# One fixed order for VectorE's steps of a slot, and another block for a held product, in a two-layer convolution-attention kernel

## The chip, the cores and the metric

The kernel runs on one core of one Trainium2 chip. The metric is the device time of one execution in microseconds, the median of several runs.

## The reference, cut to what matters

The input is x of 2 x 512 x 32 x 32, in float32. Layer 0 is an attention over 64 sampled positions in each of 8 groups of channels, with a bias from a small network on the distance between the query's place and the sampled place, and then an MLP. Layer 1 is a plain attention over the 1024 places of each image.

```python
# layer 0
q   = gconv1x1(bn(x), qw)
off = tanh(off_pw @ gelu(depthwise 6x6, stride 4, of q)) * 4      # 8 x 8 sampling points
kv  = grid_sample(bn(x), points moved by off);  k, v = gconv1x1(kv, kw), gconv1x1(kv, vw)
pos  = grid_q[:, :, None, :] - grid_kv[:, None, :, :]             # 16 (b, group) x 1024 x 64 x 2
bias = sign(pos) * log1p(abs(pos))
bias = relu(bias @ cpb_w1 + cpb_b1)                               # 2 -> 128
bias = relu(bias @ cpb_w2 + cpb_b2)                               # 128 -> 128
bias = bias @ cpb_w3 + cpb_b3                                     # 128 -> 1
attn = softmax(q k^T / 8 + bias);  x = x + out_w @ (attn v) + out_b
x = x + mlp_w2 @ gelu(mlp_w1 @ bn2(x) + mlp_b1) + mlp_b2          # 512 -> 2048 -> 512
# layer 1
q, k, v = x Wq^T + bq, x Wk^T + bk, x Wv^T + bv
x = x + (softmax(q k^T / sqrt(512)) v) Wp^T + bp
```

The part that takes most of the time is the bias network: 2 x 8 x 1024 x 64 pairs go through its 128 x 128 layer.

## The kernel before, in words

The program is written as one stream of calls. A scheduler of the framework puts them into an order for each engine by its own estimate of what is ready when; `tc.issue_after(i)` adds an edge, so that what is issued inside it stands behind instruction `i`. Each engine then runs its own stream in order.

**The slots.** The bias network is cut into NS = 256 slots, NSL = 16 of them for each of NG = 16 groups (image, chunk of channels, half). A slot is four positions times 1024 queries. Its functions are these:

- `load_tables` (L645) loads a table `fb` of 512 KB for four slots by a DMA on SyncE, and `st_tables` (L656, L664) makes `ta` and `tb` from it on ScalarE: the first layer's two terms.
- `st_layer1(s)` (L676) is the first layer: one custom VectorE instruction adds the terms and clips at zero, and gives `h` of 128 x 4096. There are three buffers of it; slot s issues that of s+2.
- `st_layer2(s)` (L693) is the 128 x 128 layer on TensorE: four tiles, z = 0 to 3, each with 8 matmuls of the program into a PSUM tile from a pool of three. ScalarE evicts them with a relu: z 0 and z 2 to `rx` (L703, three buffers), z 3 to `ub` (L705, three buffers), and z 1 (L705) to a buffer that goes by the slot's place in eight: `u8` (four buffers) for place 0, `u4` (two) for place 4, `uc` (two) for places 2 and 6, `uo` (three) for odd ones. The page calls u8 and u4 both `u`.
- `st_sum(s, 0)` and `st_sum(s, 2)` (L713) are sums on VectorE, `ub = rx * sc + ub`, 128 x 1024 each: of z 0 and 1, and of z 2 and 3. The second also issues on GpSimd's queue an adding DMA of the one into the other (L715).
- Folds, copies and joins (L732 on GpSimd's queue, L739 on SyncE's) bring the sums of two, four and eight slots together, at slots that the table `due` holds.
- `st_layer3` (L823) is the last layer, on TensorE, for all sums of a group into `sim`: for the groups that start at slots 0 to 192 it is issued 27 slots after the group's start, and reads u8 buffers; for those that start at 208 and 224 it is issued 22 slots after, at slots 230 and 246, and reads u8 and u4 buffers; that of 240 follows the loop.
- `softmax_steps` (L836 to L876) are the softmax of a group, in pieces, and `later()` gives the pieces of the chains that prepare the tables of later chunks (`CHAINS`, five of them): one piece in a slot, behind an eviction.

The loop (L886 to L940) issues in each slot, in this order: the second sum of slot s-1, the folds and joins that are due, a table's load, `st_layer1(s + 2)`, `st_layer2(s)`, a table, the first sum of slot s, and then background pieces. No edge orders VectorE's h and sums among themselves.

**The MLP.** After the loop come the output projection (`project`, L1020) and the MLP in eight units, four parts of the hidden width for each of two images. All of its products are made by a scheme of seven products of half size in place of eight. In `layer1` the scheme is used twice: `twice` (matmuls at L160) runs three sets of seven products, one after another, by times: product number q of set g has the time 7g + t, with t from `STEPS`, and calls given as `fills` stand among them by their own times. The seven blocks of `hm` (128 x 2 x 512 each) hold the results: blocks 0 to 3 `c11, c12, c21, c22`, block 4 `r5`, block 5 `r3`; set 0 goes to blocks 0 and 1, set 1 to 2 and 3, set 2 to 4 and 5. The last products are added by `plus` (L137) on VectorE, their copies and scalings are ScalarE's (L166, L170 and their like), and `gelu` (L1092) is ScalarE's. Block 6 is written by the last `spread` of `layer1`, after all sets. One product of the scheme is made plainly, in `second` (time 21), from PSUM into c11. In the first unit (`early`) it is made ahead of all sets, in `first` (time -1), and held in `r3` until `plus(c11, c11, r3)` at time 13.5; the gelu of c11 follows at 19.5. `layer2` (L1073) then multiplies hm by the second weights.

Of the kernel before, what the change touches and what calls it, by code (L numbers as in the profile page):

```python
# [57 lines left out]
def conv_seq_kernel(ctx: ExitStack, tc: tile.TileContext, x, xt, kst, pst, cst, vec, wsm, outw, w1, w2, wl, wlt, brow, out):  # L58
    nc = tc.nc
# [4 lines left out]
    def newest(engine):  # L64
        return next(i for i in reversed(nc.cur_bb.bb.instructions) if i.engine == engine)
# [70 lines left out]
    def plus(out, a, b_, op=ALU.add):  # L136
        nc.vector.tensor_tensor(out, a, b_, op)  # L137
# [69 lines left out]
    with tc.tile_pool(name="lp", bufs=2) as lp:  # L207
# [426 lines left out]

        NS = NG * NSL
        tabs, h1s, sums, sims, added = {}, {}, {}, {}, {}
        evicted, raw = {}, {}


        def load_tables(c):  # L640
            b, k, f = groups[c // 4]
            ci, kk = chain_of[b, k]
            assert ci in state
            fb = lp.tile([P, 2, W, KT], F32, name="fb", bufs=1)
            nc.sync.dma_start(  # L645
                out=fb.rearrange("p a x j -> p (a x j)"),
                in_=fdr[ci][f * len(CHAINS[ci]) + kk, c % 4].rearrange("p j -> (p j)").partition_broadcast(P),
            )
            raw[c] = fb
# [18 lines left out]
        def st_layer1(s):  # L668
            ta, tb = tabs[4 * s // KT]
            j = 4 * s % KT  # L670
            h1 = lp.tile([P, H, 4, W], F32, name="h1", bufs=3)
            a = ta[:, j : j + 4, :].rearrange("p t x -> p (t x)")
            b = tb[:, j // 4].rearrange("p y t -> p (y t)")
            step = H // 2 if s == 0 else H
            for y in range(0, H, step):
                nc.vector._custom_dve(  # L676
                    TENSOR_ADD_SAT,
                    out=h1[:, y : y + step].rearrange("p y t x -> p (y t x)"),
                    in0=a.unsqueeze(1).to_broadcast([P, step, 4 * W]),
                    in1=b[:, 4 * y : 4 * (y + step)].unsqueeze(2).to_broadcast([P, 4 * step, W]),  # L680
                    s0=FMAX, s1=0.0,
                )
            h1s[s] = h1


        def st_layer2(s):
            h1 = h1s.pop(s)
            r = []
            for z in range(4):
                ps = zp.tile([P, 2, 512], F32, name="ps2")  # L690
                for h in range(2):
                    for q in range(4):
                        nc.tensor.matmul(  # L693
                            ps[32 * q : 32 * q + 32, h, :], cw2[:, 32 * z : 32 * z + 32],
                            h1[:, 16 * h : 16 * h + 16, q, :], start=True, stop=True,
                        )
                name, bufs = (
                    ("rx", 3), (("u8", 4), ("uo", 3), ("uc", 2), ("uo", 3), ("u4", 2), ("uo", 3), ("uc", 2), ("uo", 3))[s % 8],
                    ("rx", 3), ("ub", 3),
                )[z]  # L700
                o = lp.tile([P, 2, 512], F32, name=name, bufs=bufs)
                if z % 2 == 0:
                    nc.scalar.activation(o, ps, AF.Relu, bias=sc[:, 4 + z : 5 + z])  # L703
                else:
                    nc.scalar.activation(o, ps, AF.Relu, bias=sc[:, 4 + z : 5 + z], scale=sc[:, z : z + 1])  # L705
                r.append(o)
                if z % 2 == 1:
                    evicted.setdefault(s, []).append(nc.cur_bb.bb.instructions[-1])
            sums[s] = r

        def st_sum(s, z):
            r = [t.rearrange("p h n -> p (h n)") for t in sums[s][z : z + 2]]
            nc.vector.scalar_tensor_tensor(r[1], r[0], sc[:, z : z + 1], r[1], ALU.mult, ALU.add)  # L713
            if z == 2 and s < NS - 1:
                nc.gpsimd.dma_start(out=sums[s][1], in_=sums[s][3], accum_op=ALU.add)  # L715
                added[0] = nc.cur_bb.bb.instructions[-1]
# [167 lines left out]
        st_layer1(0)  # L884
        st_layer1(1)
        for s in range(NS):  # L886
            if s > 0:
                st_sum(s - 1, 2)
            for _, go, a in sorted(due.get(s, ()), key=lambda e: e[0]):
                go(a)  # L890
            if s % 4 == 0 and s // 4 + 1 < 4 * NG:
                load_tables(s // 4 + 1)
            if s + 2 < NS:
                st_layer1(s + 2)
            st_layer2(s)


            if s % 4 == 0 and s // 4 + 1 < 4 * NG:
                with tc.issue_after(evicted[s][0]):
                    st_tables(s // 4 + 1)  # L900
            st_sum(s, 0)

            if bg is not None and (s % 4 or s < 60):
                with tc.issue_after(evicted[s][1]):
                    next(bg, None)
            if bg is not None and state.get(len(CHAINS) - 1, 0) is None:

                bg = None
                php.__exit__(None, None, None)
                opp = tc.tile_pool(name="op", bufs=1, side="right")  # L910
                op = opp.__enter__()
                op0 = op_blocks(
                    0, op.tile([P, 3, 2, 512], F32, name="op0x"), op.tile([P, 3, 2, 256], F32, name="op0w")
                )
                ready = s
            if bg is None and s > ready and (s - ready) % 4 == 0 and (s - ready) // 4 <= 8:
                i = (s - ready) // 4 - 1
                if i < 4:
                    spread(op0[1], (i,))
                else:  # L920
                    fold(nc.vector, op0[0], which=(i - 4,))

            if tails and (s % (2 if s < 60 else 4) or s >= NS - NSL):
                with tc.issue_after(evicted[s][s % 4 == 0]):
                    if next(tails[0], 0) is not None:
                        tails.pop(0)
            for t in (27, 22):
                if s % NSL == t % NSL and s >= t and (s - t < FULL) == (t == 27):
                    st_layer3(s - t)
                    tails.append(softmax_steps((s - t) // NSL))  # L930
# [37 lines left out]
    with ExitStack() as top, tc.tile_pool(name="wp", bufs=1) as wp:  # L968
# [120 lines left out]
        def layer1(p, we, w, xb, xe, hm, others=(), early=False):  # L1089
            def gelu(blk, src, scale=1.0):  # L1090
                for m in range(2):
                    nc.scalar.activation(  # L1092
                        hm[:, blk, m, :], src[:, m, :], AF.Gelu,
                        bias=col("mb1", 4 * p + 2 * (blk // 2) + m), scale=scale,
                    )

            c11, c12, c21, c22, r5, r3 = (hm[:, j] for j in range(6))

            def weights(q, j):
                a = FIRST_W[PARTS[q][0]]  # L1100
                return [inner_w(w, we, a, a - 1)[j]]

            def moving(q, j):
                b_ = FIRST_X[PARTS[q][1]]
                return [inner_x(xb, xe, b_, b_ - 1)[j]]

            def dest(g, m, h):
                return hm[:, 2 * g : 2 * g + 2, m, 256 * h : 256 * h + 256]

            def done(g):  # L1110
                if g == 0:
                    plus(c12, c12, c11)
                elif g == 1:
                    plus(c22, c22, c12)
                    plus(c21, c21, c22)
                    gelu(2, c21, -1.0)
                else:
                    plus(c22, c22, r5)
                    gelu(3, c22, -1.0)
                    plus(c12, c12, r5)  # L1120
                    plus(c12, c12, r3)
                    gelu(1, c12)

            def second():
                ps = mq.tile([P, 2, 512], F32, tag="ps2", name="sw")
                product(w, xb)(ps, 0, 0)
                plus(c11, c11, ps)
                gelu(0, c11)

            def first():  # L1130
                ps = mq.tile([P, 2, 512], F32, tag="ps2", name="sw")
                product(w, xb)(ps, 0, 0)
                nc.scalar.copy(r3, ps)

            plain = ((21, second),)
            if early:
                plain = (-1, first), (13.5, lambda: plus(c11, c11, r3)), (19.5, lambda: gelu(0, c11))
            twice(mq, ((1, 6), (4, 7), (5, 3)), weights, moving, dest, done, (*plain, *others))
            spread([hm[:, j] for j in range(7)])

# [52 lines left out]
        for i, (b, p) in enumerate(units):  # L1193
# [10 lines left out]
            hm = cp.tile([P, 7, 2, 512], F32, tag="big", name="hm")  # L1204
# [387 lines left out]
```

## Time and profile before

| | us |
|---|---|
| median of 3 runs | 2620.16 |
| lowest, highest | 2619.61, 2620.79 |
| the profiled execution, its own time | 2620.51 |
| its span | 2618.7 |
| TensorE's matmuls busy | 2596.1 (99%) |
| VectorE busy | 2310.0 (88%) |
| ScalarE busy | 1746.8 (67%) |
| GpSimd busy | 981.0 (37%) |
| mean granted TensorE clock | 0.999 |

The span is the stretch from the first to the last instruction in the record of the profiled execution; 1.8 us of the execution lie around it. A group of instructions is written as line, engine, operation, out<-in with partitions x elements, count, then busy time in us, mean ns of one, and the idle time of the engine just before them with what ended most of it. A row of the waits says which engine at which line waited for which, the sum in us, how many times, and the longest. A row of the timeline has the start, the duration in us, the engine, the line and the operation, and in brackets the idle time ahead of it and who ended it. One matmul of the program shows as two in the records of the slots. In the trace, slot 228 starts on TensorE at 1683.93 us, slot 232 at 1715.02, slot 246 at 1814.76, and slot 255 at 1882.82.

### The profile page before, as it was taken

To read this page: it belongs to the slowest core of one execution; us is meant where nothing else is said; L and a number is where in the kernel's file an instruction comes from. 1 tells how busy PE (TensorE), PEld (TensorE's weight loads), DVE (VectorE), ACT (ScalarE), POOL (GpSimd) and SP (SyncE) were. 2 spreads that over 40 slices of the span, in tenths; PEclk is the share of its full clock that TensorE was granted. 3 is DMA by queue.
4 is the path that set the end of the run, shared out by engine and by line. 5 is a ranking of instruction groups with operands and counts; after the bars stand their busy time and mean duration, and the time that the engine had idled before them with its cause. 6 is when DMAs were issued, how large, how long until landed. Compare 5 with 4: busy or idle time off the path is not lost.

```text
span 2618.7 us, 48901 instructions
## 1 busy us (share of the span) xinstructions
PE 2596.1 (99%) x19648; PEld 1003.4 (38%) x19648; DVE 2310.0 (88%) x1462; ACT 1746.8 (67%) x2325; POOL 981.0 (37%) x1121
## 2 busy tenths in 40 slices
PE   9999999999999999999999999999999999999999
PEld 3332322233233233323333332332355665646556
DVE  7999999999999999999999999998876587666656
ACT  5887888888887888888887777777733242314041
POOL 1344544444445444444454444333332334200100
PEclk9999999999999999999999999999999999999999
DMA  5888988999899998899898999787787768400202
GB/s 188 173 192 187 212 183 183 195 199 199 190 193 193 187 205 196 179 192 198 187 202 176 201 191 192 164 182 170 150 210 166 153 140 172 94 16 1 73 0 57
DMA packets 177522, 428.27 MB, mean 164 GB/s; under 512 B 29936, under 2 KB 78208, under 8 KB 174608
## 3 DMA queue, kind: packets, MB, share of 16 engines
q0 software_dynamic: 107392, 273.09, 58.2%
q1 hardware_dynamic: 69472, 151.75, 17.5%
q8 instruction: 155, 2.54, 0.4%
q14 instruction: 71, 0.58, 0.1%
q10 hardware_dynamic: 432, 0.31, 0.0%
HBM read 82.16 MB, written 6.55 MB: 34 GB/s over the span
## 4 chain that ended last, share of the span: by engine, by line
PE 67%; DVE 12%; issue 9%; DMA 6%; POOL 4%; ACT 2%; DVEq 0%; SPq 0%; POOLq 0%; ACTq 0%
PE ps L693 39%; PE sw L1073 7%; PE sw L160 7%; PE sw L1242 7%; DVE h L676 4%; DMA u<-uc 3%; DVE ub L713 2%; POOL u L732 2%; PE sw L1020 2%; PE sw L1340 2%; PE psg L595 1%; DVE uo L713 1%; DMA u<-uo 1%; PE sim L823 1%; DMA u<-u 1%
## 5 line engine op out<-in xcount | busy, mean ns | idle before, releaser
L693 PE MATMUL ps<-h,cw 128*32 128x512 f32 x16384 | 1775.4, 593 | 11.1 <-ACT rx L703 7.9
L676 DVE CUSTOM_DVE_ANT_1 h<-ta,tb 128x4096 f32<-128x4096 f32 (+1 forms) x257 | 1130.5, 4400 | 20.6 <-PE ps L693 16.8
L693 PEld LDWEIGHTS ps<-h,cw 128*32 128x32 f32 x16384 | 525.9, 110 | 1229.7 <-issue 1132.2
L703 ACT ACTIVATE rx<-ps,sc 128x1024 f32<-128x1024 f32 x512 | 568.2, 1110 | 158.0 <-PE ps L693 99.1
L732 POOL DMA_DIRECT2D u<-u x397 | 410.0, 1516 | 14.5 <-DMA u<-ub 12.0
L705 ACT ACTIVATE ub<-ps,sc 128x1024 f32<-128x1024 f32 x256 | 308.3, 1204 | 84.1 <-PE ps L693 82.4
L713 DVE SCALAR_TENSOR_TENSOR ub<-rx,sc,ub 128x1024 f32<-128x1024 f32 x256 | 326.7, 1276 | 10.5 <-ACT ub L705 10.5
L715 POOL DMA_DIRECT2D uo<-ub x127 | 112.1, 883 | 586.0 <-DVE ub L713 538.6
L1073 PE MATMUL sw<-hm,w2t 128*128 128x512 f32 x448 | 194.4, 593 | 0.3 <-DVE hm L125 0.2
L705 ACT ACTIVATE uo<-ps,sc 128x1024 f32<-128x1024 f32 x128 | 154.1, 1204 | 42.7 <-PE ps L693 41.3
L713 DVE SCALAR_TENSOR_TENSOR uo<-rx,sc,uo 128x1024 f32<-128x1024 f32 x128 | 163.4, 1277 | 5.0 <-ACT uo L705 5.0
L732 POOL DMA_DIRECT2D u<-uc x126 | 126.9, 1272 | 19.5 <-DMA u<-uc 18.3
L715 POOL DMA_DIRECT2D uc<-ub x64 | 56.3, 879 | 200.6 <-DVE ub L713 159.7
L1073 PEld LDWEIGHTS sw<-hm,w2t 128*128 128x128 f32 x448 | 84.8, 190 | 104.4 <-issue 97.4
L137 DVE TENSOR_TENSOR hm<-hm,sw 128x512 f32<-128x512 f32 x79 | 57.6, 732 | 74.1 <-PE sw L160 51.7
L715 POOL DMA_DIRECT2D u<-ub x64 | 55.1, 860 | 172.0 <-DVE ub L713 168.2
L732 POOL DMA_DIRECT2D uc<-uc x63 | 108.5, 1722 | 2.1 <-DMA uc<-ub 2.1
L732 POOL DMA_DIRECT2D uc<-uo x63 | 103.3, 1639 | 15.3 <-DMA uc<-uo 15.3
L1406 POOL DMA_DIRECT2D xs<-rs x6 | 7.2, 1200 | 258.6 <-DVE rs L137 258.6
L732 POOL DMA_DIRECT2D u<-uo x63 | 87.3, 1386 | 19.4 <-DMA u<-uo 14.8
L705 ACT ACTIVATE uc<-ps,sc 128x1024 f32<-128x1024 f32 x64 | 77.0, 1203 | 24.5 <-PE ps L693 18.0
L656 ACT ACTIVATE ta<-fb,vs 128x512 f32<-128x512 f32 (+1 forms) x65 | 88.7, 1368 | 6.6 <-DMA fb<-fdr 6.6
(295 smaller groups left out, 2622.4 us busy)
## 6 DMA issues: line engine op xcount, KB each, us to landing
uo<-ub POOLq DMA_DIRECT2D x127, 512.0 KB, 5.3
fb<-fdr SPq DMA_DIRECT2D x64, 512.0 KB, 5.8
u<-ub POOLq DMA_DIRECT2D x64, 512.0 KB, 6.5
uc<-ub POOLq DMA_DIRECT2D x64, 512.0 KB, 6.0
u<-u POOLq DMA_DIRECT2D x63, 256.0 KB, 6.9
u<-uo SPq DMA_DIRECT2D x63, 256.0 KB, 5.9
u<-uo POOLq DMA_DIRECT2D x63, 256.0 KB, 7.4
uc<-uc POOLq DMA_DIRECT2D x63, 256.0 KB, 8.2
```

Source lines behind the costliest of these rows:

```text
L137: nc.vector.tensor_tensor(out, a, b_, op)
L160: nc.tensor.matmul(bank[:, e, :], w, x, start=(q in (1, 2, 5) and e == k == 0), stop=True, skip_group_check=True,)
L656: nc.scalar.activation(ta.rearrange("p j x -> p x j")[:, :, j0:j1], fb[:, 0, :, j0:j1], AF.Identity, bias=col("cb1"), scale=col("w1x"),)
L676: nc.vector._custom_dve(TENSOR_ADD_SAT, out=h1[:, y : y + step].rearrange("p y t x -> p (y t x)"), in0=a.unsqueeze(1).to_broadcast([P, ste ...
L693: nc.tensor.matmul(ps[32 * q : 32 * q + 32, h, :], cw2[:, 32 * z : 32 * z + 32], h1[:, 16 * h : 16 * h + 16, q, :], start=True, stop=True,)
L703: nc.scalar.activation(o, ps, AF.Relu, bias=sc[:, 4 + z : 5 + z])
L705: nc.scalar.activation(o, ps, AF.Relu, bias=sc[:, 4 + z : 5 + z], scale=sc[:, z : z + 1])
L713: nc.vector.scalar_tensor_tensor(r[1], r[0], sc[:, z : z + 1], r[1], ALU.mult, ALU.add)
L715: nc.gpsimd.dma_start(out=sums[s][1], in_=sums[s][3], accum_op=ALU.add)
L732: nc.gpsimd.dma_start(out=out, in_=in_, accum_op=ALU.add)
L1073: nc.tensor.matmul(ps[:, m, :], w[:, a, k, m * P : (m + 1) * P], x[:, b_, k, :], start=(k == 0), stop=(k == 1),)
L1242: nc.tensor.matmul(ps[:, m, :], w[:, a, k, c + m * P : c + (m + 1) * P], x[b_][:, k, :], start=(k == 0), stop=(k == nk - 1),)
```

## The change

In the loop, `st_layer1(s + 2)` is issued first and the second sum of slot s-1 after it; the three steps of a slot on VectorE, h of s+2, second sum of s-1, first sum of s, are chained by edges, each behind the newest of them. The edges concern VectorE's order alone. In the first MLP unit the held product goes to block 6 of hm and not to block 5; the plus and the gelu of c11, at times 13.5 and 19.5 before, become one call at time 21.

```diff
@@ the loop over the slots
         for s in range(NS):
+            if s + 2 < NS:
+                with tc.issue_after(summed[-1]) if summed else nullcontext():
+                    st_layer1(s + 2)
+                    summed.append(newest(mybir.EngineType.DVE))
             if s > 0:
-                st_sum(s - 1, 2)
+                with tc.issue_after(summed[-1]):
+                    st_sum(s - 1, 2)
+                    summed.append(newest(mybir.EngineType.DVE))
...
-            if s + 2 < NS:
-                st_layer1(s + 2)
             st_layer2(s)
...
-            st_sum(s, 0)
+            with tc.issue_after(summed[-1]):
+                st_sum(s, 0)
+            summed.append(newest(mybir.EngineType.DVE))
@@ layer1
             def first():
                 ps = mq.tile([P, 2, 512], F32, tag="ps2", name="sw")
                 product(w, xb)(ps, 0, 0)
-                nc.scalar.copy(r3, ps)
-
-            plain = ((21, second),)
-            if early:
-                plain = (-1, first), (13.5, lambda: plus(c11, c11, r3)), (19.5, lambda: gelu(0, c11))
+                nc.scalar.copy(hm[:, 6], ps)
+
+            def merge():
+                plus(c11, c11, hm[:, 6])
+                gelu(0, c11)
+
+            plain = ((-1, first), (21, merge)) if early else ((21, second),)
```

More of the change, by code (lines that the diff above doesn't have):

```diff
@@ L636, in conv_seq_kernel @@
         tabs, h1s, sums, sims, added = {}, {}, {}, {}, {}
-        evicted, raw = {}, {}
+        evicted, raw, summed = {}, {}, []
         def load_tables(c):
```

## The prediction

> **What bounds the kernel now.** I read the engines' busy time first, then the costliest groups, then TensorE's waits.
>
> ```profile
> PE 2596.1 (99%) x19648; PEld 1003.4 (38%) x19648; DVE 2310.0 (88%) x1462; ACT 1746.8 (67%) x2325; POOL 981.0 (37%) x1121
> ...
> L693 PE MATMUL ps<-h,cw 128*32 128x512 f32 x16384 | 1775.4, 593 | 11.1 <-ACT rx L703 7.9
> L676 DVE CUSTOM_DVE_ANT_1 h<-ta,tb 128x4096 f32<-128x4096 f32 (+1 forms) x257 | 1130.5, 4400 | 20.6 <-PE ps L693 16.8
> ...
> L713 DVE SCALAR_TENSOR_TENSOR ub<-rx,sc,ub 128x1024 f32<-128x1024 f32 x256 | 326.7, 1276 | 10.5 <-ACT ub L705 10.5
> ```
>
> TensorE is the bound: 2596.1 of 2618.7 us. A slot's 64 matmuls take 1775.4 / 256 = 6.94 us. VectorE does one h (4.40) and two sums (1.28 each by their rows; 1.20 by start to start, since they overlap by about 0.08) in a slot: 6.75 us, or 97%. So TensorE sets the pace, and VectorE, once late, gains back only some 0.15 us a slot. The waits of TensorE say how little is to be had:
>
> ```profile
> PE ps L693 <- ACT rx L703: 7.9, 14, 1.9
> ...
> PE ps L693 <- DVE h L676: 1.4, 2, 0.7
> PE sw L160 <- ACT hm L166: 1.2, 1, 1.2
> ```
>
> The first two rows are 9.3 us, and TensorE's timeline places 3.5 us of them at two spots: 1713.7 (0.71) and 1808.1 to 1831.0 (0.54, 1.89, 0.70); by the pitch of matmul starts, where 0.425 us is the usual step, these and two smaller gaps are about 1.1 and 3.6, together 4.7 us. The last row is one stall at 1962.4, in the first MLP unit. VectorE's timeline shows the first spot:
>
> ```profile
> 1684.18 4.43 DVE L676 CUSTOM_DVE_ANT_1 h<-ta,tb 128x4096 f32<-128x4096 f32 x1 [0.91 <-PE ps L693]
> 1688.53 1.28 DVE L713 SCALAR_TENSOR_TENSOR ub<-rx,sc,ub 128x1024 f32<-128x1024 f32 x1
> 1691.05 4.43 DVE L676 CUSTOM_DVE_ANT_1 h<-ta,tb 128x4096 f32<-128x4096 f32 x1 [1.25 <-PE ps L693]
> ...
> 1708.74 1.28 DVE L713 SCALAR_TENSOR_TENSOR u<-rx,sc,u 128x1024 f32<-128x1024 f32 x1 [1.14 <-ACT u L705]
> 1710.45 8.76 DVE L676 CUSTOM_DVE_ANT_1 h<-ta,tb 128x4096 f32<-128x4096 f32 x2 [0.43 <-ACT tb L664]
> ```
>
> These are slots 228 to 233. The line at 1708.74 is the sum of z 0 and 1 of slot 228, owed since about 1690, and 1710.45 is h of slots 232 and 233, for which TensorE waits at 1714.3. Why that sum is so late, ScalarE and TensorE tell:
>
> ```profile
> 1707.50 1.21 ACT L705 ACTIVATE u<-ps,sc 128x1024 f32<-128x1024 f32 x1 [0.74 <-PE sim L823]
> ```
>
> The eviction of slot 228's z 1 goes into one of only two u4 buffers, and waits until layer 3 of group 208 (L823, 1705.53 to 1707.45) has read what slot 212 left in it. The same happens at slot 244 (eviction at 1824.76, released by L823 of group 224). These are the only two: earlier groups read only u8 in layer 3.
>
> [...] nothing is put ahead of the sum at 1708.74, and the two h start right after it and the table. [...]
>
> **The change, part by part.** No instruction is added or removed in the loop. The fixed order is h(s+2), sum ub(s-1), sum of z 0,1 of s. I compared the built order of both kernels on each engine. On VectorE they differ at the start, slots 56 to 60, 110 to 115, 143, 164, 227 to 240 and 243 to 255; everywhere else it was this order already.
>
> *Slots 227 to 240.* Before: h230, ub227, h231, ub228, uo229, ub229, uc230, ub230, u4 of 228, h232. After: h230, ub227, **u4 of 228**, h231 and so on. A step that waits for a buffer now stands four sums and one h earlier, and all of VectorE queues behind it. TensorE's and ScalarE's streams move to suit: layer 3 of group 208 starts after slot 229, not 230, split around tile 230.0, and the eviction of u4 stands ahead of rx of 229.2. I walked it with the trace's durations (a tile 1.72 us, 0.25 from a tile's end to its eviction, eviction 1.1 to 1.2, a layer-3 matmul pair of the source 0.21): ub227 ends 1689.8; slot 229 ends on TensorE 1697.7; five layer-3 steps to 1698.75; tile 230.0 waits for the PSUM tile that ub of 229.3 leaves at 1699.15, ends 1700.87; the three u4 steps end 1701.5; eviction 1701.75 to 1702.96; the sum starts at 1703.0. VectorE idles 1689.8 to 1703.0 = 13.2 us. Before, between the same two h it idled 1.25 + 1.29 + 2.44 + 2.15 + 1.14 + 0.43 = 8.7 us. So +4.5 us of VectorE, at 97% load. Of this 0.5 is eaten by the sums that still were owed before: h236 ends at 1737.8 instead of 1734.97 with one more sum owed, about 4.0. TensorE has no slack to swallow it, as slot 232 waited for h already: slot 232 starts at about 1718.6, not 1715.02 (+3.6), slot 234 at 1733.4, not 1729.48 (+3.9).
>
> *Slots 243 to 255.* The same with u4 of 244: idle of VectorE 1811.9 to 1822.4, 10.5 us, against 7.9 before (+2.6). Slot 248 starts 0.7 us later still (+4.7 in all); of that 0.5 comes back, since the stall of 0.53 at 1880.1 is covered. End of loop about **+4.2**. So the 4.7 us of stalls there aren't saved; they become about 8.7. Bounds of the two together: -4.7 (both stalls vanish) to +7.1 (4.5 + 2.6, nothing absorbed).
>
> *Slots 56 to 60.* h runs ahead of ub and uo by one step: a sum comes 4.4 us later, and with it the release of its rx buffer (of three). TensorE loses about **+0.6** (0 to 1.2). *110 to 115:* a stall of about 1.2 is worked out, but the three stalls that follow it in before (0.5, 0.26, 0.4) go in exchange: **0** (0 to +0.6). *Start, 143, 164:* one pair of steps changes places where VectorE was ahead; 0, hidden by h two slots ahead; uncovered, at most one sum, 1.2 us.
>
> *DMAs that move with the sums.* The POOL add of ub into u4 (L715, 0.88 us of issue, 6.5 to land) of 228 and 244 goes ahead of those of uo and uc; one table load on SP changes places with two copies of 256 KB. Their next readers are the copies and joins seven slots (48 us) on, and a table one chunk ahead: 0, hidden. Uncovered: the joins behind land later, one add each, up to 2 x 1.5 us.
>
> *MLP unit 0.* The copy of the first product goes to block 6 instead of block 5, so the copy of the third set (L166, blocks 4 and 5) need not wait for the plus that reads block 5 (1961.48, 1.22 us). The stall of 1.16 us (1.38 by pitch) goes. No plus or gelu is added. But the q7 scaling of set 2 now comes behind the table load (1.28) and the gelu, and the plus at 21 behind these: I estimate 0.5 to 0.6 back. **-0.8** (-1.4 to 0).
>
> Sum: 4.2 + 0.6 - 0.8 = +4.0; I take off 0.2 for what other stalls of the loop absorb (by pitch they hold some 18 us more): **+3.8**. The profiled execution is 2620.51 us (span 2618.7, 1.8 around it), 0.35 above the median; 2620.2 + 3.8 = **2624.0**. From no change a measurement of this kernel can tell about 0.2%, 5.24 us: 2614.9 to 2625.4 counts as the same.
>
> **Rivals.** *Faster.* The fixed order does what it was drawn for: h is never behind a sum, so the waits for h and rx at both spots go: -4.7 - 0.8 = -5.5, 2614.7, or 2614.2 if the 0.53 at 1880.1 goes too: about 2614.4. It decides from the point where u4's eviction is ready when VectorE comes to the sum, that is layer 3 of group 208 over by 1689. Against it: that layer reads a join which landed only at 1699.1. *An even trade.* VectorE's idle only moves: the same stalls, unit 0 gains: 2619.5. For it: layer 3 is one slot earlier. Against: +4.5 us idle by the walk. *Slower than the bound.* Layer 3 now stands so early that it waits for joins still in flight (the one for 236 landed at 1816.0 before; TensorE would come to it at about 1814), and the whole of VectorE and ScalarE's evictions queue behind it: up to +7.1 with no absorption, 2627.5. It decides from about 2 us of DMA wait before L823.
>
> **How the numbers follow.** Forecast 0.50 (2621 to 2627; 0.12 of it above 2625.4), even trade 0.22, faster 0.12 (0.02 of it within the bound), slower 0.16. Range 2617 to 2628.5: it leaves out the faster case and a little of the slower one. Faster 0.10, same 0.62, slower 0.28.
>
> **What would show it.** Right: VectorE idle ahead of the u sums of slots 228 and 244 of about 13 and 10 us, released by ACT u, itself by PE sim L823; slot 232 at about 1718.6; the row PE sw <- ACT hm gone. Wrong: those idles below 8 us, or TensorE's waits at ps L693 fewer than 9.3 us in all.

## The result, and the profile after

The changed kernel takes 2628.77 us (median of 6 runs, 2628.22 to 2631.12), beside 2620.46 of the kernel before in the same runs: a ratio of 1.0033, 95% interval 1.002 to 1.0046. That is +8.3 us where +3.8 was forecast, just outside the range (2628.5). The profiled execution has a span of 2627.0 us, 8.3 more than before.

The page after, the busy times and the groups that were shown of before:

```profile
PE 2599.0 (99%) x19648; PEld 1001.8 (38%) x19648; DVE 2306.9 (88%) x1462; ACT 1745.8 (66%) x2325; POOL 978.3 (37%) x1121
...
L693 PE MATMUL ps<-h,cw 128*32 128x512 f32 x16384 | 1777.0, 593 | 14.4 <-ACT rx L703 9.3
L676 DVE CUSTOM_DVE_ANT_1 h<-ta,tb 128x4096 f32<-128x4096 f32 (+1 forms) x257 | 1130.7, 4400 | 20.0 <-PE ps L693 16.1
...
L713 DVE SCALAR_TENSOR_TENSOR ub<-rx,sc,ub 128x1024 f32<-128x1024 f32 x256 | 326.9, 1277 | 4.1 <-ACT ub L705 4.1
```

Work and durations are the same. Idle time ahead of the bias network's matmuls is 14.4 us and not 11.1, and VectorE's wait ahead of the ub sums fell from 10.5 to 4.1. Where it went, VectorE's waits say:

```profile
DVE u L713 <- ACT u L705: 27.2, 5, 13.4
```

Before, that row was 5.1 us in 6 waits, the longest 1.6. VectorE's timeline has the two places:

```profile
1688.77 1.27 DVE L713 SCALAR_TENSOR_TENSOR ub<-rx,sc,ub 128x1024 f32<-128x1024 f32 x1
1703.48 1.29 DVE L713 SCALAR_TENSOR_TENSOR u<-rx,sc,u 128x1024 f32<-128x1024 f32 x1 [13.43 <-ACT u L705]
1704.68 4.42 DVE L676 CUSTOM_DVE_ANT_1 h<-ta,tb 128x4096 f32<-128x4096 f32 x1
...
1811.23 1.27 DVE L713 SCALAR_TENSOR_TENSOR ub<-rx,sc,ub 128x1024 f32<-128x1024 f32 x1
1824.22 1.28 DVE L713 SCALAR_TENSOR_TENSOR u<-rx,sc,u 128x1024 f32<-128x1024 f32 x1 [11.72 <-ACT u L705]
1825.43 4.42 DVE L676 CUSTOM_DVE_ANT_1 h<-ta,tb 128x4096 f32<-128x4096 f32 x1
```

One long hole stands where before there were six short ones. ScalarE's timeline names who ends it, and TensorE's shows layer 3 (L823) split around a tile, and the waits behind it:

```profile
1702.24 1.21 ACT L705 ACTIVATE u<-ps,sc 128x1024 f32<-128x1024 f32 x1 [2.88 <-PE sim L823]
...
1822.99 1.20 ACT L705 ACTIVATE u<-ps,sc 128x1024 f32<-128x1024 f32 x1 [4.31 <-PE sim L823]
```

```profile
1699.42 2.08 PE L693 MATMUL ps<-h,cw 128*32 128x512 f32 x16
1701.16 1.03 PE L823 MATMUL sim<-u,w3f 128*32 128x512 f32 x6
1702.13 1.08 PE L804 MATMUL sim<-qa,kz 64*64 64x512 f32 x4
1703.50 1.92 PE L693 MATMUL ps<-h,cw 128*32 128x512 f32 x16 [0.29 <-ACT u L705]
1706.24 3.64 PE L693 MATMUL ps<-h,cw 128*32 128x512 f32 x32 [0.81 <-ACT rx L703]
1711.20 0.66 PE L840 MATMUL pt<-ident,ss 128*128 128x128 f32 x4 [1.33 <-ACT ub L705]
...
1899.12 1.05 PE L823 MATMUL sim<-u,w3f 128*32 128x512 f32 x4 [1.78 <-issue]
```

The last line is the layer 3 after the loop, which waited 0.32 before. What it waits for the profile does not name, but in both traces it starts 2.63 us after GpSimd's queue issued the last join into `u`. Before:

```profile
1887.56 0.82 POOL L732 DMA_DIRECT2D u<-uc  x1 [5.32 <-DMA u<-uc]
1890.19 1.05 PE L823 MATMUL sim<-u,w3f 128*32 128x512 f32 x4 [0.32 <-issue]
```

After, that join came 8.93 us later, as layer 3 did:

```profile
1896.49 0.82 POOL L732 DMA_DIRECT2D u<-uc  x1 [4.90 <-DMA u<-uc]
```

From the start times of the slots on TensorE in both traces, the delay of after against before is (us):

| slot 0 | slot 58 | slot 60 | slot 70 | slot 229 | slot 232 | slot 238 | slot 246 | slot 255 | layer 3 after the loop | after MLP unit 0 |
|---|---|---|---|---|---|---|---|---|---|---|
| -0.56 | -0.68 | +0.75 | +0.20 | +0.24 | +4.08 | +5.20 | +3.97 | +7.45 | +8.93 | +8.31 |

So slots 56 to 60 cost 1.4; the first place 5.0 (229 to 238), the second 2.2 (238 to 255), the loop's end 1.5; the MLP unit gives 0.6 back. Two entries belong to the one execution of before and not to the change: the -0.56 ahead of slot 0 (other kernels had -0.6 to +0.1 there), and the 0.55 that comes back between slots 60 and 70, where the kernels below that keep the order of before gain 0.3 to 0.6 on it too.

### The profile page after: what moved, and what is told of

It reads as the page before. It is cut to its first block, busy times and chain, and to the rows that moved or that the text cites. A ratio compares the mean times of both kernels' runs of the same rounds, so it can differ in the third digit from the quotient of the medians.

```text
span 2627.0 us, 48906 instructions
## 1 busy us (share of the span) xinstructions
PE 2599.0 (99%) x19648; PEld 1001.8 (38%) x19648; DVE 2306.9 (88%) x1462; ACT 1745.8 (66%) x2325; POOL 978.3 (37%) x1121
## 4 chain that ended last, share of the span: by engine, by line
PE 68%; DVE 11%; issue 10%; DMA 6%; POOL 3%; ACT 2%; DVEq 0%; POOLq 0%; ACTq 0%; SPq 0%
PE ps L693 41%; PE sw L1079 7%; PE sw L160 7%; PE sw L1250 7%; DVE h L676 3%; DMA u<-uc 3%; DVE ub L713 3%; POOL u L732 2%; PE sw L1026 2%; PE sw L1348 2%; PE psg L595 1%; DMA u<-u 1%; PE sim L823 1%; DVE uo L713 1%; DMA uc<-uo 1%
## 5 line engine op out<-in xcount | busy, mean ns | idle before, releaser
L693 PE MATMUL ps<-h,cw 128*32 128x512 f32 x16384 | 1777.0, 593 | 14.4 <-ACT rx L703 9.3
L693 PEld LDWEIGHTS ps<-h,cw 128*32 128x32 f32 x16384 | 523.7, 110 | 1235.1 <-issue 1129.1
L713 DVE SCALAR_TENSOR_TENSOR u<-rx,sc,u 128x1024 f32<-128x1024 f32 x64 | 81.8, 1277 | 27.4 <-ACT u L705 27.2
L705 ACT ACTIVATE u<-ps,sc 128x1024 f32<-128x1024 f32 x64 | 77.1, 1204 | 27.4 <-PE ps L693 18.0
```

Of the source, the lines that this page charges most:

```text
L693: nc.tensor.matmul(ps[32 * q : 32 * q + 32, h, :], cw2[:, 32 * z : 32 * z + 32], h1[:, 16 * h : 16 * h + 16, q, :], start=True, stop=True,)
```

## The experiments

Theory A is the prediction's: VectorE stands behind a buffer that layer 3 still reads. B says that the fixed order costs as such, all along the loop. C says that the rearranged streams of TensorE and ScalarE cost, not VectorE's. Times stand beside those of the kernel before on the same chip.

**The MLP part alone.** The second half of the diff on the kernel before.

> The kernel before with only the second part of the change: the held product of unit 0 in block 6, plus and gelu at time 21. Theory A (the loss is VectorE's queue standing behind a u4 buffer at slots 228 and 244; this part gains what the trace after shows, 8.93 us of delay at the loop's end falling to 8.27 after the unit): 2619.8 us, 0.7 below before. Rival B (the loss has to do with the order in general and the MLP part is empty): 2620.5. A loss here would be against both.

2620.29 us beside 2620.87; ratio 0.9999 (0.999 to 1.0007). The time alone can't tell it from nothing. The trace can: the row PE sw <- ACT hm L166 of 1.2 us is gone, and the delay against before falls by 0.62 over the unit. It is a small gain, and the loss is elsewhere.

**Edges up to slot 199 only.** All three `issue_after` of the loop are given only for a range of slots:

```diff
-                with tc.issue_after(summed[-1]):
+                with tc.issue_after(summed[-1]) if s < 200 else nullcontext():
                     st_sum(s - 1, 2)
```

> The changed kernel, but the edges between VectorE's steps hold only in slots 0 to 199; from 200 on the scheduler orders the sums itself. VectorE's order at slots 227 to 255 is then nearly that of before (the u4 sum of 228 behind ub of 230), all else as changed. Theory A: the 3.7, 3.5 and 1.5 us of slots 228, 244 and the loop's end go, 0.8 of slots 56 to 123 and the MLP's -0.7 stay: 2620.5 us. Rival B (h ahead of the ub sum in every slot holds rx buffers and costs all along the loop): 2625 or more, since 200 of 256 slots keep that order.

2622.05 beside 2620.87; ratio 1.0003 (0.9995 to 1.0012). The run before has the same MLP part and no edges and took 2620.29, so the fixed order in 200 of 256 slots costs some 1.8 us; in the traces 1.4 of it sits in slots 58 to 60. B holds for that much and falls for the rest: most of the loss is in the last 56 slots.

**The fixed order, without the wait.** Slot 228 takes a u8 buffer; every later u4 then finds a free one, slot 244's too:

```diff
-    ("rx", 3), (("u8", 4), ..., ("uo", 3))[s % 8],
+    ("rx", 3), (("u8", 4), ..., ("uo", 3))[s % 8 * (s != 228)],
```

> The changed kernel with its fixed order throughout; the only edit is that slot 228's z 1 goes to a u8 buffer (four of them) instead of a u4 one, so that neither the u4 of 228 nor that of 244 has to wait for layer 3. Theory A: VectorE's idle before those two sums is under 1.5 us, and the stalls that before had there (4.7 us) go as well: 2620.5 - 4.7 + 0.8 - 0.7 = 2615.9 us. Rival B: the order is the same, so 2626 to 2629. Rival C (the loss sits in the streams of TensorE and ScalarE that were rearranged around layer 3): 2622 to 2628, as layer 3 stays split.

> The kernel before with the same single edit, slot 228's z 1 in a u8 buffer; no edges, MLP as before. The built order on VectorE at slots 227 to 255 is then the fixed one of the change, by the scheduler's own choice. Theory A: 2620.5 - 4.7 = 2615.8 us. Rival B (that order is the loss): 2626 or more. Rival C: between 2620 and 2626.

2614.91 and 2614.34 beside 2620.87; ratios 0.9977 (0.9969 to 0.9985) and 0.9974 (0.9965 to 0.9983). VectorE of the fixed order with the u8 buffer:

```profile
1690.40 1.28 DVE L713 SCALAR_TENSOR_TENSOR ub<-rx,sc,ub 128x1024 f32<-128x1024 f32 x1
1691.59 1.28 DVE L713 SCALAR_TENSOR_TENSOR u<-rx,sc,u 128x1024 f32<-128x1024 f32 x1
1692.92 4.43 DVE L676 CUSTOM_DVE_ANT_1 h<-ta,tb 128x4096 f32<-128x4096 f32 x1
```

It is the same sequence as in the changed kernel, with no hole, and 14 us faster: the h behind the u sum, which started at 1704.68 there, starts at 1692.92. So at the two places the order is harmless once the buffer is free, and the wait for the buffer is the cost: A holds. The order is not quite free elsewhere: with the same buffer and the MLP part but no edges, the last run of this section is 7.23 us below before, and this one 5.96, so that the edges cost about 1.3 us. C is not tried by it, since layer 3 came back whole (one piece at 1707.10) when the buffer was free. In the kernel before the same edit gains 6.5 us, more than the 4.7 of stalls that I had counted there: by slots it gains 4.1 up to 246, 1.5 to 255 and 0.5 at the loop's end.

**The sums elsewhere in the order.** First, the u4 sums of 228 and 244 outside the chain:

```diff
-            with tc.issue_after(summed[-1]):
+            if s in (228, 244):
                 st_sum(s, 0)
-            summed.append(newest(mybir.EngineType.DVE))
+            else:
+                with tc.issue_after(summed[-1]):
+                    st_sum(s, 0)
+                summed.append(newest(mybir.EngineType.DVE))
```

> The changed kernel, but the u4 sums of slots 228 and 244 stand outside the chain of edges. In the built order they move back by one h and two sums (h231, ub228, uo229, u4 of 228, h232), and layer 3 moves back to the end of slot 230, so that u4's eviction comes at about 1707.5 again. Theory A (what counts is how long VectorE stands idle before that sum): it arrives at about 1697.2 and waits to 1708.7, some 11.5 us against 13.4 in the changed kernel and 8.7, spread over six steps, before: about 2.3 us lost at each place, 2625.5 us. Rival C (the early, split layer 3 is what costs): 2620.5 us, since layer 3 is where it was before.

2629.29 beside 2620.18; ratio 1.0034 (1.0021 to 1.0047). Layer 3 was not split around a tile of the network here and stood after slot 230, as before; still the time is that of the changed kernel. C falls as far as it rests on layer 3's place. A's number was missed by 4, and the trace has two reasons. The first is the idle time of VectorE at the first place, where I had expected 11.5 us:

```profile
1691.32 4.43 DVE L676 CUSTOM_DVE_ANT_1 h<-ta,tb 128x4096 f32<-128x4096 f32 x1 [1.25 <-PE ps L693]
...
1709.83 1.28 DVE L713 SCALAR_TENSOR_TENSOR u<-rx,sc,u 128x1024 f32<-128x1024 f32 x1 [11.69 <-ACT u L705]
1711.57 4.42 DVE L676 CUSTOM_DVE_ANT_1 h<-ta,tb 128x4096 f32<-128x4096 f32 x1 [0.46 <-ACT tb L664]
```

1.25 + 11.69 + 0.46 = 13.4 us, as much as in the changed kernel. The second is TensorE's pace. Behind a wait of 2.30 us at the first place the matmuls of a slot, 64 records, took longer than behind no wait or a short one:

```profile
1709.48 7.07 PE L693 MATMUL ps<-h,cw 128*32 128x512 f32 x64
...
1719.86 8.66 PE L693 MATMUL ps<-h,cw 128*32 128x512 f32 x64 [2.30 <-ACT ub L705]
1729.16 7.07 PE L693 MATMUL ps<-h,cw 128*32 128x512 f32 x64 [0.63 <-ACT rx L703]
```

8.66 in place of 7.07 us cost 1.6 us here. For the second place, whose wait is 3.6 us, I put 1.5: an estimate, from the 1.5 to 1.7 that waits with slow matmuls behind them cost in these traces (the table in the last section). The mean granted clock of this execution reads 0.998, that of the changed kernel's 0.999. In the changed kernel no wait of the loop's tiles is longer than 1.7 us, a slot behind one of 0.92 took 7.07, and the granted clock is 1.00 from 20 to 2600 us. So the equal times are in part chance: by slots the first place cost 7.0 us here against 5.0, or 5.4 without the slow slot, the second 1.8 against 2.2, or 0.3 without it, and the loop's end gave 0.5 back where the changed kernel lost 1.5. And the last wait of VectorE's listing names a second thing behind u4's eviction, the table of slots 232 to 235 (`st_tables` is issued behind the eviction of z 1 of slot 228). The next two runs put the sum two slots later, for both slots and for 228 alone:

```diff
-            with tc.issue_after(summed[-1]):
-                st_sum(s, 0)
-            summed.append(newest(mybir.EngineType.DVE))
+            for a in ([] if s in (228, 244) else [s]) + ([s - 2] if s in (230, 246) else []):
+                with tc.issue_after(summed[-1]):
+                    st_sum(a, 0)
+                summed.append(newest(mybir.EngineType.DVE))
```

> The changed kernel, but the u4 sums of 228 and 244 are issued two slots later, chained behind the first sum of 230 and 246: h231, ub228, uo229, h232, ub229, uc230, u4 of 228, h233. Theory A: VectorE comes to it at about 1704, idles some 5 us, less than the 8.7 of before, and h232 is made in time: about 2618 us, idle before each u sum under 6 us. Rival B (the fixed order as such): 2626 or more. Rival C: 2620.5.

> As the run before, but for slot 228 alone; the u4 sum of 244 stays early as in the changed kernel. It prices the second place alone, the term that the prediction put at +0.7. Theory A: the place costs 3.5 us and 1.5 at the loop's end whatever happened at the first: 2623.5 us, with about 11.7 us idle before the u sum of 244. Rival D (the second place is dear only because VectorE comes to it late from the first): under 2620.

2645.70 and 2640.04 beside 2620.18; ratios 1.0095 (1.0078 to 1.0111) and 1.0073 (1.0058 to 1.0088): far off every expectation. VectorE with both sums late:

```profile
1713.22 4.42 DVE L676 CUSTOM_DVE_ANT_1 h<-ta,tb 128x4096 f32<-128x4096 f32 x1 [13.39 <-ACT tb L664]
...
1728.87 1.28 DVE L713 SCALAR_TENSOR_TENSOR u<-rx,sc,u 128x1024 f32<-128x1024 f32 x1 [8.83 <-issue]
```

Two waits, neither of which I had seen. h232 now comes before the sum, and waits 13.39 us for the table behind the same eviction. And the sum now stands in the program behind the fold of slot 228 (due at slot 230), an adding DMA on the same buffer, and starts at 1728.87. The profile names no releaser for its wait; the u<-u DMAs were issued from 1719.67 to 1721.27, and with the 6.9 us to landing that are their median in the kernel before they landed by about 1728, an estimate. Its place in the program changed what it depends on, and by the program's order also what is computed: the fold adds one half of the lanes to the other before `rx * sc` has come in. In both runs TensorE was also slow behind a wait: 16 matmul records took 3.58 us behind one of 2.64 us, and 3.52 behind one of 2.67, where the 16 at 1716.13 and 1714.38 took 1.92. So these two runs don't price the place that they were made for, and the second one says nothing clean of slot 244.

**The second place alone.** Slot 244 instead of 228 takes a u8 buffer (`s != 244` in the edit above).

> The changed kernel, but slot 244's z 1 (not slot 228's) goes to a u8 buffer: the first place keeps its wait, the second loses it. It prices the second place, the term that the prediction put at +0.7. Additive: by the traces the second place is 5.0 us in slots 246 to 255 and 2.0 at the loop's end between waiting and not waiting, so 2628.8 - 7.0 = 2621.8 us. Rival D (part of the stall after slot 246 is inherited from the first place, so that it stays): 2625. If the prediction's +0.7 were right (against stalls of 3.6 that before had there): 2628.8 - 4.3 = 2624.5, with the first place dearer than it was put.

2625.60 beside 2620.55; ratio 1.0019 (1.0011 to 1.0026). The total looks like rival D, but the slots do not: from 238 to 255 the delay falls by 4.4 us, against a rise of 2.2 in the changed kernel, so the second place's wait is worth 6.6 in the loop. It is given back after the loop, where layer 3 waits 3.2 us and then runs at half pace:

```profile
1894.58 1.92 PE L823 MATMUL sim<-u,w3f 128*32 128x512 f32 x4 [3.19 <-issue]
1896.26 1.83 PE L823 MATMUL sim<-u,w3u 128*32 128x512 f32 x4
```

The four records of the first line took 1.05 us in the changed kernel, behind a wait of 1.78. What layer 3 waits for is the chain of last copies and joins: on GpSimd's queue the join uc<-uo started at 1884.46 after 7.5 us of waiting for a copy that SyncE had issued at 1878.58. With slot 228's edit the same copy took 3.0 us from issue to join, and layer 3 did not wait. Why it took 5.9 here isn't settled. Not every execution pays for the half pace. Eight records from start to start took 3.33 us here and 1.72 in the changed kernel, so 1.6 us are lost. If a lower granted clock is what it was, this is 0.0006 of the span, and the mean would read 0.999 at most (an estimate). The three of the 17 runs whose mean reads 1.0 took 2623.2 to 2623.8 us, the other 14 2625.1 to 2627.2.

**The table.** The tables of slots 232 and 248 are made behind the last eviction of slot 227 and 243:

```diff
-                with tc.issue_after(evicted[s][0]):
+                with tc.issue_after(evicted[s - 1][1] if s in (228, 244) else evicted[s][0]):
                     st_tables(s // 4 + 1)
```

On the changed kernel; on it with the sums outside the chain; on the kernel before:

> The changed kernel, but the tables of slots 232 and 248 are made on ScalarE behind slot 227's and 243's last eviction, not behind u4's eviction of 228 and 244. VectorE's order is that of the changed kernel, the u4 sum ahead of h231. Theory A (the sum's place holds VectorE): no change, 2628.8 us, and 13 us idle before the u sum. Rival E (it is the table behind the eviction that holds VectorE, as the run with the sums two slots later showed for h232): 2624 or less.

> The same, and the u4 sums of 228 and 244 outside the chain, as in the run with the sums in the middle. The built order puts them behind h233 and behind ub of 246; every other step keeps the fixed order. Theory A with the table: both things that stood behind the eviction are out of VectorE's way, its idle time at each place is under 5 us and the stalls of before go too: 2616 us. Rival B (the fixed order as such) 2626 or more; if the table doesn't matter, 2629 as in the middle run.

> The kernel before with the tables of slots 232 and 248 behind slot 227's and 243's last eviction; nothing else. If the stalls that before had at the two places (4.7 us) came from the table behind u4's eviction: 2615.5 us. If they came from the late sums and rx buffers: within 1 us of 2620.5.

2629.82, 2619.78 and 2618.88 beside 2620.55; ratios 1.0035 (1.0022 to 1.0048), 0.9995 (0.9986 to 1.0003) and 0.9996 (0.9987 to 1.0004). In the changed kernel the sum alone holds VectorE, so the table changes nothing, and rival E falls. With the sum free to move, the table is worth 9.5 us (2629.29 to 2619.78, from two sets of runs with 2620.18 and 2620.55 for before): only then have both things left the eviction's shadow. About 3.1 of the 9.5 are the slow slots of the two places (1.6 measured and 1.5 estimated), which went with the waits. In the loop both of the last two did what was expected: from slot 229 to 255 they gain 5.0 us on the kernel before. Then the loop's end takes most of it again, by a wait and half the pace behind it, here in the kernel before with early tables:

```profile
1886.29 1.89 PE L823 MATMUL sim<-u,w3f 128*32 128x512 f32 x4 [2.42 <-issue]
1887.90 1.98 PE L823 MATMUL sim<-u,w3u 128*32 128x512 f32 x4
```

With the sums outside the chain, four of the twelve runs have a mean granted clock that reads 1.0, and so, by the estimate above, none of this half pace: they took 2616.8 to 2617.9, near the 2616 expected; the other eight took 2619.0 to 2621.4.

**The parts that gain, without the edges.** The kernel before with slot 228 in u8 and the MLP part.

> The kernel before with slot 228's z 1 in a u8 buffer and the change's MLP part, no edges: the parts that gain without those that cost. Theory A: 2620.5 - 6.5 (as the run with the u8 buffer showed) - 0.7 = 2613.3 us, or 0.6 to 0.7 below the run with the u8 buffer alone.

2612.95 beside 2620.18; ratio 0.9971 (0.9959 to 0.9983). It is the fastest of all: 7.2 us below before, of which 0.7 is the MLP part (6.5 for the buffer alone, against its own runs of before).

## Why the prediction was wrong

The mechanism was right: the places, the chain VectorE u sum, ScalarE u eviction, TensorE layer 3, and the idle time at the first place (13.2 forecast, 13.43 measured), and slot 232's delay (3.6 forecast, 3.8 measured from slot 229). Four terms of the sum were too small.

- *Slots 227 to 240*: put at 3.9 once slot 234 is reached; 4.5 there, and 5.0 by slot 238, past the last slot that the forecast read.
- *Slots 243 to 255*, "slot 248 starts 0.7 us later still", of which 0.5 was to come back: 2.2 measured. This is the step that failed worst. VectorE's extra idle time there was put at 10.5 - 7.9 = 2.6 and was 11.72 - 7.9 = 3.8, and of those 2.6 only 0.7 was let through to TensorE, on the ground that before had stalls there which would be exchanged. Of the measured 3.8, 2.2 came through. The two places together measured 5.0 + 2.2 = 7.2 us, as much as the prediction's bound without absorption (7.1), but that is chance: VectorE's extra idle time had grown from 7.1 to 4.7 + 3.8 = 8.5, and 7.2 of it came through.
- *The joins behind the sums* were put at "0, hidden", with 2 x 1.5 us if uncovered. At the loop's end a join was uncovered: layer 3 waited 1.78 us and not 0.32, and the delay grew by 1.5 us. It was the last join of the loop and not one right behind the two sums. That join came 8.9 us later than before while slot 255 came 7.45 later; why it fell back further than TensorE is not shown. The rival "slower than the bound" named a wait of layer 3 for joins in flight, but at slots 230 and 246; in the changed kernel it came at the loop's end instead, and only the run with the sum of slot 228 alone late has it at slot 246 (3.1 us).
- *Slots 56 to 60* were put at +0.6, 0 to 1.2, and cost 1.4, in this trace and in each of the others with the same program order.

With the first three, 3.8 + (5.0 - 3.9) + (2.2 - 0.3) + 1.5 = 8.3. (0.3 is what the +4.2 left for the second place.) That this meets the measured number is luck in part: what the small terms missed, 0.8 at slots 56 to 60, 0.2 in the MLP unit and the 0.2 taken off, is cancelled by the two entries that belong to the one execution of before, 0.56 and 0.55.

Some of the prediction's small figures are slips that its sum does not rest on: the four gaps that it lists for TensorE's two spots add up to 3.84 and not 3.5, the times that it gives for the end of h236 are starts, 4.7 of stalls and +4.2 make 8.9 and not 8.7, and 2620.2 + 7.1 is 2627.3.

The other steps held. 110 to 115: 0 forecast, and a stall of 1.6 there was taken back by slot 124. MLP unit: -0.8 forecast, a stall of 1.3 gone and 0.7 given back. The rival "faster" was right on one thing: the stalls at the two places can be had, and 6.5 us with them, but by a buffer and not by an order.

What stays open: why the copy ahead of the last joins sometimes takes 3 us longer at the loop's end; and whether layer 3's split costs anything of its own, since no run had the split without the wait.

## What to carry to other kernels

A fixed order on an engine is only as good as the one step in it that can wait for something far away (13.43 us here): before fixing an order, list what each step waits for, at every place in the loop and not only in its steady part, and give the step that waits a free buffer first. On a second engine that is 97% busy, count extra idle time at nearly its full size: here 7.2 of 8.5 us came through within the loop. And look at everything that stands behind the same release: here two steps, the sum and a table, stood behind one eviction, and moving only one of them gained nothing. Look at the pace of the matmuls behind the longest waits, too: here a slot took 1.6 us more behind a wait of 2.30 us, and 7.08 us, as usual, behind one of 1.89 in the kernel before.

## What the runs showed of the hardware

VectorE took its steps in the order of its stream: the h behind the u sum started at 1704.68 us, after the 13.43 us for which the sum waited, and at 1692.92 in the same order with the buffer free. The table load beside the gelu of MLP unit 0, which the prediction counts, took 1.28 us in the trace of before (ACT L1092, at 1963.49).

Seven waits of TensorE from 2.30 us up, and what the matmul records behind them took (behind three more, of 3.1, 3.2 and 3.6 us, it is not shown):

| kernel | wait, us | records behind it | us | the same number elsewhere, us |
|---|---|---|---|---|
| sums outside the chain | 2.30 | 64 of L693 | 8.66 | 7.07, same trace |
| both sums late | 2.64 | 16 of L693 | 3.58 | 1.92, same trace |
| the sum of 228 late | 2.67 | 16 of L693 | 3.52 | 1.92, same trace |
| before, tables early | 2.42 | 4 of L823 | 1.89 | 1.05, changed kernel |
| sums outside the chain, tables early | 2.81 | 4 of L823 | 1.92 | 1.05, changed kernel |
| slot 244 in u8 | 3.19 | 4 of L823 | 1.92 | 1.05, changed kernel |
| both sums late | 2.96 | 4 of L823 | 1.05 | 1.05, changed kernel |

Behind six of the seven the matmuls were slow, behind the one of 2.96 us they were not. Behind waits of 0.3, 1.0 and 1.78 us ahead of the last layer 3 four records took 1.05. In the six, the wait cost 1.5 to 1.7 us more than its length: 1.59, 1.66 and 1.60 in the first three rows, and in the next three, over eight records from start to start, 3.2 to 3.3 us in place of 1.72. The length of the wait alone does not tell which of these seven are slow.
